# A gather-weighted adapter with residual and layer norm on one core: other shares of the b2 additions for three engines, and another order at the end

## The chip, the core and the metric

The kernel runs on one core of one Trainium2 chip. The core has five engines with a queue of instructions each: PE (TensorE, matmul), DVE (VectorE), ACT (ScalarE), GpSimd (POOL in the profile) and SP (SyncE, which here only issues transfers). They run side by side and wait for one another through semaphores. Sixteen DMA engines move data between device memory and the on-chip memory SBUF. Matmul results land in PSUM, a second on-chip memory of eight banks of 128 x 512 float32 values. The metric is the device time of one execution in microseconds. The kernel before takes 311.26 us (median of 3 runs, 311.04 to 311.28).

## What is computed

For each of 128 batches there is a block `x[b]` of 128 rows by 512 columns in float32, and a language number `v = itok[b]` from 0 to 8. Ten languages have their own weights.

```python
h       = relu(x[b] @ W1[v] + b1[v])             # 128 x 128
y       = x[b] + h @ W2[v] + b2[v]               # 128 x 512
mean    = mean of y over the 512 columns
var     = mean of (y - mean)^2 over the columns
out[b]  = x[b] + (y - mean) * rsqrt(var + 1e-5) * gamma[v] + beta[v]
```

All inputs and the output are float32.

## The kernel before

One batch fills the 128 partitions with its 128 rows. All weights stay in SBUF; at the start the rows of `beta`, `gamma` and `b2` are spread over all partitions by small matmuls (`spread`), so that `beta_b`, `gamma_b` and `b2_b` hold a 128 x 512 block for each language. Gamma is stored times -0.5, which the last step of the root below needs.

A batch passes through these steps, named by the functions of the code and the lines of the profile:

- `transpose_x` (L232, PE): four 128 x 128 transposes into the PSUM tile `pxT`; `copy_xT` (L236, ACT) brings it to SBUF.
- `stage_w1` (L223, ACT) copies the batch's W1 into the tile `w1s`; `down` (L255, PE) multiplies; `relu` (L263, ACT) makes `hT`.
- `up` (L272, PE) multiplies with W2 into the PSUM tile `py`, one of five buffers.
- `b2` is added in one of three ways. `add_b2` (L242, GpSimd) writes `r = x + b2` ahead of time, into a ring of four SBUF tiles. Or `vector_b2` (L282, DVE) adds it to `py` in PSUM. Or `up` puts a small matmul in front (L271, PE) that starts `py` with the b2 row. `b2_by_matmul(b)` and `b2_by_vector(b)` decide; what neither takes goes to GpSimd.
- `residual` (L289, DVE) adds `r` or `x` to `py`, with the row sums as a second result; `negative_means` (L303, DVE) turns the sums of two batches into means.
- `square` (L312, ACT) takes the sum of squared deviations, and `deviation` (L322, ACT) an approximate reciprocal root of it, for two batches at once. `rstd` (L326, L328, L331, DVE) refines that root by one Newton step in three small instructions.
- `scale` (L355, DVE): `py = (py - mean) * gamma`, and `finish` (L364, DVE): `o = py * rstd + o`, where `add_beta` (L249, GpSimd) has put `o = x + beta` before. Finishing a batch frees its `py` buffer for the batch five later.
- `store` (L368, SP) writes two batches.

The order is written out by hand: `keep` chains every instruction behind the one before it on its engine, so each engine runs exactly in program order. In the main loop, iteration `i` works on several batches at once: PE transposes batch `i`, runs `down` for `i - 1` and `up` for `i - 2`; DVE takes the residual of `b = i - 3`, finishes batch `b - 3` and scales batches of the pair before; GpSimd makes `r` for `b + 2` and `o` for `b`.

All roots lie in one PSUM tile, `small`: columns 0 and 1 are zeros, which `negative_means` adds as its second operand, and other columns take the roots of two pairs in turn and of the last four single batches. The framework tracks what waits for what by tiles.

The last batches go another way. `E` is 123; from batch 124 on `tail(b)` writes out the order by hand, with roots for single batches (`deviation_of`, L395 and L322; `rstd_of`, again L326, L328, L331). Batches 123 and 124, and the left half of 125, are finished by ACT and GpSimd together (`by_pool`: ACT at L409 computes `py * rstd`, with the mean's part from `shift`, L403, as bias where gamma is still to come; GpSimd multiplies by gamma at L411 and adds `o` at L413). The rest is finished by DVE (`finish_cols`, L420). All of GpSimd's remaining beta additions stand ahead of its first `by_pool` instruction in its queue. The last six batches are stored one by one (`store_last`, L416), in the order 122 to 127 on SP's queue.

Of the kernel before, what the change touches and what calls it, by code (L numbers as in the profile page):

```python
# [8 lines left out]
FP = mybir.dt.float32  # L9
# [3 lines left out]
ALU = mybir.AluOpType  # L13
# [3 lines left out]
P = 128  # L17
G = 4
EPS = 1e-5
# [6 lines left out]
def cond_resid_kernel(ctx: ExitStack, tc: tile.TileContext, x, itok, W1, b1, W2, b2, gamma, beta, out):  # L26
# [8 lines left out]
    nc = tc.nc  # L35
    B, S, H = x.shape
# [8 lines left out]
    def keep(ins):  # L45

        engine = ins.ins.engine
        if engine in last:
            tc.add_manual_dep(ins.ins, last[engine], behind, reason="kept order")
        last[engine] = ins.ins.name  # L50
        return ins
# [4 lines left out]
    op = ctx.enter_context(tc.tile_pool(name="op", bufs=5))  # L56
    tp = ctx.enter_context(tc.tile_pool(name="tp", bufs=2))
    wp = ctx.enter_context(tc.tile_pool(name="wp", bufs=5))
    st = ctx.enter_context(tc.tile_pool(name="st", bufs=6))
    p_x = ctx.enter_context(tc.tile_pool(name="p_x", bufs=1, space=PSUM))  # L60
    p_h = ctx.enter_context(tc.tile_pool(name="p_h", bufs=1, space=PSUM))
    p_s = ctx.enter_context(tc.tile_pool(name="p_s", bufs=1, space=PSUM))
# [3 lines left out]
    E = B - 5  # L66
# [6 lines left out]
    def xb(b):  # L73
        return xs[b // G][:, b % G, :]
# [57 lines left out]
    def lid(b, engine):  # L132
        g = b // G
        if (g, engine) not in lids:
            loads, vals = nc.values_load_multi_w_load_instructions(
                lang[0:1, g * G : (g + 1) * G],
                engines=[engine],
                min_val=0,
                max_val=L - 1,
                skip_runtime_bounds_check_because="clamped on the chip to 0..L-1 above",  # L140
            )
            for ins in loads:
                keep(ins)
            lids[g, engine] = vals
        return lids[g, engine][b % G]
# [65 lines left out]
    xT, hT, rs, os, ys, ssqs, nmeans, rstds = {}, {}, {}, {}, {}, {}, {}, {}  # L211
    phs, pxs, sums = {}, {}, {}

    def b2_by_matmul(b):
        return b < 4 or (b % 4 == 1 and not b2_by_vector(b) and b < E)

    def b2_by_vector(b):
        return b % 4 == 1 and (b % 8 == 5 if b < 24 else b % 32 != 1) and 8 <= b < B - 8

    def stage_w1(b):  # L220
        w1s[b] = wp.tile([P, KC, A], FP, tag="w1s", name=f"w1s_{b}")
# [53 lines left out]
    def col(tiles, b):  # L275

        return tiles[b // 2][:, b % 2 : b % 2 + 1]
# [6 lines left out]
    def residual(b):  # L284
        r = rs.pop(b) if b in rs else xb(b)
        if b % 2 == 0:
            sums[b // 2] = st.tile([P, 2], FP, tag="sum", name=f"sum_{b // 2}")
        keep(
            nc.vector.scalar_tensor_tensor(ys[b], ys[b], 1.0, r, ALU.mult, ALU.add, accum_out=col(sums, b))  # L289
        )  # L290


    small = {}

    def smalls(lo, n):
        if not small:
            small["t"] = p_s.tile([P, 64], FP, tag="s", name="small")
            keep(nc.vector.memset(small["t"][:, 0:2], 0.0))
        return small["t"][:, lo : lo + n]

    def negative_means(g):
        nmeans[g] = st.tile([P, 2], FP, tag="nmean", name=f"nmean_{g}")
        keep(nc.vector.scalar_tensor_tensor(nmeans[g], sums[g], -1.0 / H, smalls(0, 2), ALU.mult, ALU.add))  # L303

    def square(b):

# [10 lines left out]
    H3 = float(H) ** 3  # L317
# [3 lines left out]
    def root(ssq, t):  # L321
        keep(nc.scalar.activation(t, ssq, AF.Abs_reciprocal_sqrt, bias=eps, scale=1.0 / H3))  # L322

    def newton(n, ssq, t, u):
        if n == 1:
            keep(nc.vector.scalar_tensor_tensor(u, ssq, EPS * H3, t, ALU.add, ALU.mult))  # L326
        else:
            keep(nc.vector.scalar_tensor_tensor(u, u, 1.0 / H3, t, ALU.mult, ALU.mult))  # L328

    def newton_3(rstd, t, u):  # L330
        keep(nc.vector.scalar_tensor_tensor(rstd, u, -3.0, t, ALU.add, ALU.mult))  # L331

    parts_of = {}

    def of_pair(g):
        if g not in parts_of:
            parts_of[g] = smalls(8 + 8 * (g % 2), 2), st.tile([P, 2], FP, tag="part", name=f"part_{g}")
        return parts_of[g]

    def deviation(g):  # L340
# [2 lines left out]
    def rstd(g, n):  # L343
        t, u = of_pair(g)
        if n < 3:
            newton(n, ssqs[g], t, u)
        else:
            rstds[g] = st.tile([P, 2], FP, tag="rstd", name=f"rstd_{g}")
            newton_3(rstds[g], t, u)
            del ssqs[g], parts_of[g]  # L350

    def scale(b):
        v = lid(b, ET.DVE)
        keep(
            nc.vector.scalar_tensor_tensor(  # L355
                ys[b], ys[b], col(nmeans, b), gamma_b[:, bass.ds(v * H, H)], ALU.add, ALU.mult
            )
        )

    def finish(b):  # L360
        g, j = divmod(b, 2)
        o = os[g][:, j, :]
        keep(
            nc.vector.scalar_tensor_tensor(o, ys.pop(b), rstds[g][:, j : j + 1], o, ALU.mult, ALU.add)  # L364
        )

    def store(g):
        keep(nc.sync.dma_start(out=out[2 * g : 2 * g + 2].rearrange("b s h -> s b h"), in_=os.pop(g)))  # L368
        del rstds[g]
# [5 lines left out]

    shifts = {}

    def of_one(b):
        if -b not in parts_of:
            parts_of[-b] = smalls(32 + 8 * (b % 4), 1), st.tile([P, 1], FP, tag="part", name=f"part_of_{b}")  # L380
        return parts_of[-b]

    def rstd_of(b, n):

        t, u = of_one(b)
        if n < 3:
            newton(n, ssqs[b], t, u)
        else:
            rstds[b] = st.tile([P, 1], FP, tag="rstd", name=f"rstd_{b}")
            newton_3(rstds[b], t, u)  # L390

    def deviation_of(b):
        ssqs[b] = st.tile([P, 1], FP, tag="ssq", name=f"ssq_{b}")
        sq = tp.tile([P, H], FP, tag="sq", name=f"sq_{b}")
        keep(nc.scalar.activation(sq, ys[b], AF.Square, bias=col(sums, b), scale=-float(H), accum_out=ssqs[b]))  # L395
        root(ssqs[b], of_one(b)[0])

    def rstd_col(b):
        return rstds[b] if b > E else rstds[b // 2][:, b % 2 : b % 2 + 1]

    def shift(b):
        shifts[b] = st.tile([P, 1], FP, tag="shift", name=f"shift_{b}")
        keep(nc.vector.tensor_scalar(shifts[b], col(nmeans, b), rstd_col(b), None, ALU.mult))  # L403

    def by_pool(b, scaled, cols=slice(0, H)):

        n = rp.tile([P, H], FP, tag="r", name=f"n_{b}")[:, cols]
        bias = 0.0 if scaled else shifts[b]
        keep(nc.scalar.activation(n, ys[b][:, cols], AF.Identity, bias=bias, scale=rstd_col(b)))  # L409
        if not scaled:  # L410
            keep(nc.gpsimd.tensor_tensor(n, n, gamma_b[:, bass.ds(lid(b, ET.Pool) * H, H)], ALU.mult))  # L411
        o = os[b // 2][:, b % 2, cols]
        keep(nc.gpsimd.tensor_tensor(o, n, o, ALU.add))  # L413

    def store_last(b):
        nc.sync.dma_start(out=out[b], in_=os[b // 2][:, b % 2, :])  # L416

    def finish_cols(b, cols=slice(0, H)):
        o = os[b // 2][:, b % 2, cols]
        keep(nc.vector.scalar_tensor_tensor(o, ys[b][:, cols], rstd_col(b), o, ALU.mult, ALU.add))  # L420

    def tail(b):
        p = E // 2
        residual(b)
        if b == E + 1:
            rstd(p, 1)
            scale(E - 1)
            rstd(p, 2)
            finish(E - 2)
            store(p - 1)  # L430
            rstd(p, 3)
            deviation_of(b)
            shift(E)
            by_pool(E, False)
        elif b == E + 2:
            rstd_of(b - 1, 1)
            negative_means(b // 2)
            rstd_of(b - 1, 2)
            finish_cols(E - 1)
            store_last(E - 1)  # L440
            rstd_of(b - 1, 3)
            store_last(E)
            deviation_of(b)
        elif b == E + 3:
            left, right = slice(0, H // 2), slice(H // 2, H)
            shift(b - 2)
            by_pool(b - 2, False)
            residual(b + 1)
            store_last(b - 2)
            rstd_of(b - 1, 1)  # L450
            scale(b - 1)
            rstd_of(b - 1, 2)
            negative_means(b // 2)
            deviation_of(b)
            scale(b)
            rstd_of(b - 1, 3)
            deviation_of(b + 1)
            by_pool(b - 1, True, left)
            rstd_of(b, 1)
            scale(b + 1)  # L460
            rstd_of(b, 2)
            finish_cols(b - 1, right)
            store_last(b - 1)
            rstd_of(b, 3)
            rstd_of(b + 1, 1)
            finish_cols(b)
            store_last(b)
            rstd_of(b + 1, 2)
            rstd_of(b + 1, 3)
            finish_cols(b + 1)  # L470
            store_last(b + 1)
# [46 lines left out]
    for i in range(3, B + U):  # L518
        b = i - U - 1
# [25 lines left out]
        g, half = divmod(b, 2)  # L545
# [80 lines left out]
```

## Time and profile before

| | |
|---|---|
| median of 3 runs | 311.26 us |
| the profiled execution's own time | 311.25 us |
| its span in the profile | 309.4 us |
| PE busy | 298.0 us, 1845 instructions |
| DVE busy | 296.2 us, 827 |
| ACT busy | 280.1 us, 716 |
| GpSimd busy | 281.4 us, 235 |
| b2 by GpSimd (L242) | 94 batches, mean 1279 ns |
| b2 by DVE (L282) | 23 batches, mean 692 ns |
| b2 by PE (L271) | 11 batches, mean 380 ns |
| moved by the DMA engines | 77.58 MB, mean 251 GB/s |

Times in the profile are microseconds from the span's start. A line of the timeline has the start, the duration, the engine, the source line, the operation, what it writes and reads by the program's names, and in brackets how long the engine was idle before it and what ended that. Instructions of one engine can overlap a little: a duration runs to the last write, and the next instruction starts earlier, so the distance from start to start is what an instruction costs its engine. A line of the list of waits has the engine and line that waited, what it waited for, and then the sum in us, the number of times and the longest. PEld is PE's loading of weights, which overlaps the matmuls; POOL is GpSimd; SPq is SP's queue of transfers.

### The profile page before, as it was taken

The numbers are of one execution on the slowest core, as the hardware profiler recorded it, in microseconds if no ns is written. First come the engines' busy times: TensorE is split into PE (matmuls) and PEld (weight loads), VectorE is DVE, ScalarE is ACT, GpSimd is POOL, SyncE is SP. The second block draws the span as 40 slices with busy tenths as digits, with TensorE's granted clock in tenths as the row PEclk, the third lists the DMA queues.
The fourth block names the chain that finished last, engine by engine and source line by source line (L and its number), as shares of the span: only waits on it lengthen the run. The fifth ranks groups of instructions, "written<-read, shape, count | busy, mean of one in ns | idle before, by whom it ended". The sixth has DMA issues, their size and how long they took to land. (4 is left out here: it accounts for less than half of the span.)

```text
span 309.4 us, 6966 instructions
## 1 busy us (share of the span) xinstructions
PE 298.0 (96%) x1845; PEld 222.1 (72%) x1845; DVE 296.2 (96%) x827; ACT 280.1 (91%) x716; POOL 281.4 (91%) x235
## 2 busy tenths in 40 slices
PE   8999999999999999999999999999999999999970
PEld 3758778787777777777777777777777777777740
DVE  6787999999999999999999999999999999999994
ACT  3857999999999999999999999999999999999991
POOL 1349999999999999999999999999999999999893
PEclk9999999999999999999999999999999999999995
DMA  7999979986677766666876766677765766882244
GB/s 232 390 387 387 374 225 370 375 278 232 230 271 267 243 210 225 222 233 239 271 249 219 246 202 246 228 250 271 249 225 203 244 237 222 263 271 106 111 159 170
DMA packets 43481, 77.58 MB, mean 251 GB/s; under 512 B 1930, under 2 KB 7061, under 8 KB 43443
## 3 DMA queue, kind: packets, MB, share of 16 engines
q1 hardware_dynamic: 43382, 77.10, 71.9%
q8 instruction: 15, 0.25, 0.3%
q14 instruction: 24, 0.19, 0.2%
q10 hardware_dynamic: 60, 0.05, 0.1%
HBM read 43.58 MB, written 33.55 MB: 249 GB/s over the span
## 5 line engine op out<-in xcount | busy, mean ns | idle before, releaser
L249 POOL TENSOR_TENSOR o<-x,beta_b 128x512 f32<-128x512 f32 x128 | 162.2, 1279 | 9.4 <-DVE beta_b L209 9.4
L255 PE MATMUL ph<-xT,w1s 128*128 128x128 f32 x1024 | 135.4, 275 | 0.0
L242 POOL TENSOR_TENSOR r<-x,b_b 128x512 f32<-128x512 f32 x94 | 120.2, 1279 | 13.1 <-DVE b_b L209 6.2
L272 PE MATMUL py<-w,hT 128*128 x256 | 132.0, 598 | 0.0
L255 PEld LDWEIGHTS ph<-xT,w1s 128*128 128x128 f32 x1024 | 124.9, 192 | 1.0 <-ACT hT L263 0.5
L232 PEld LDWEIGHTS pxT<-ident,x 128*128 128x128 f32 x512 | 66.6, 152 | 65.3 <-issue 35.4
L355 DVE SCALAR_TENSOR_TENSOR py<-py,nmean,gamma_b 128x512 f32<-128x512 f32 x126 | 95.0, 754 | 0.1
L364 DVE SCALAR_TENSOR_TENSOR o<-py,rstd,o 128x512 f32<-128x512 f32 x122 | 91.0, 746 | 0.0
L312 ACT ACTIVATE sq<-py,sum 128x512 f32<-128x512 f32 x124 | 85.2, 687 | 6.1 <-DVE py L289 6.1
L232 PE MATMUL pxT<-ident,x 128*128 128x128 f32 x512 | 78.0, 275 | 0.0
L236 ACT COPY xT<-pxT 128x512 f32<-128x512 f32 x128 | 75.1, 587 | 1.2 <-PE pxT L232 1.2
L289 DVE SCALAR_TENSOR_TENSOR py<-py,r 128x512 f32<-128x512 f32 x94 | 65.1, 693 | 1.4 <-PE py L272 0.7
L223 ACT COPY w1s<-w 128x512 f32 x104 | 63.6, 612 | 0.1
L263 ACT ACTIVATE hT<-ph,b1T 128x128 f32<-128x128 f32 x128 | 47.4, 370 | 6.4 <-PE ph L255 4.3
L272 PEld LDWEIGHTS py<-w,hT 128*128 128x128 f32 x256 | 39.6, 191 | 2.8 <-issue 0.9
L312 ACT ACTIVATION_READ_ACCUMULATOR sq<-py,sum 128x1 f32 x124 | 25.6, 206 | 0.0
L289 DVE SCALAR_TENSOR_TENSOR py<-py,x 128x512 f32<-128x512 f32 x34 | 23.8, 699 | 1.4 <-issue 0.8
L322 ACT ACTIVATE small<-ssq,eps 128x2 f32<-128x2 f32 (+1 forms) x66 | 17.5, 265 | 2.3 <-DVE nmean L303 0.2
L282 DVE TENSOR_TENSOR py<-py,b_b 128x512 f32<-128x512 f32 x23 | 15.9, 692 | 0.0
L289 DVE DVE_READ_ACCUMULATOR py<-py,r 128x1 f32 x94 | 13.3, 142 | 0.0
L326 DVE SCALAR_TENSOR_TENSOR part<-ssq,small 128x2 f32<-128x2 f32 x62 | 9.4, 152 | 1.8 <-ACT small L322 1.8
L223 ACT COPY w1s<-w1e 128x512 f32 x16 | 9.8, 613 | 1.2 <-DMA w1e<-in_L_cond_W_dram 1.1
(54 smaller groups left out, 97.4 us busy)
## 6 DMA issues: line engine op xcount, KB each, us to landing
out_dram<-o SPq DMA_DIRECT2D x61, 512.0 KB, 3.3
x<-in_x_dram SPq DMA_DIRECT2D x29, 1024.0 KB, 6.3
x<-in_x_dram SPq DMA_DIRECT2D x6, 512.0 KB, 8.9
w1e<-in_L_cond_W_dram SPq DMA_DIRECT2D x2, 1280.0 KB, 11.6
w<-in_L_cond_W_dram SPq DMA_DIRECT2D x4, 640.0 KB, 7.5
w1s<-in_L_cond_W_dram SPq DMA_DIRECT2D x8, 256.0 KB, 8.4
w<-in_L_cond_W_dram SPq DMA_DIRECT2D x1, 1792.0 KB, 10.1
out_dram<-o SPq DMA_DIRECT2D x6, 256.0 KB, 2.0
```

Of the source, the lines that this page charges most:

```text
L223: keep(nc.scalar.copy(w1s[b].rearrange("p k a -> p (k a)"), src))
L232: keep(nc.tensor.transpose(pxs[b][:, k, :], cols, ident))
L236: keep(nc.scalar.copy(xT[b], pxs.pop(b)))
L242: keep(nc.gpsimd.tensor_tensor(rs[b], xb(b), b2_b[:, bass.ds(v * H, H)], ALU.add))
L249: keep(nc.gpsimd.tensor_tensor(os[g][:, j, :], xb(b), beta_b[:, bass.ds(v * H, H)], ALU.add))
L255: nc.tensor.matmul(phs[b], lhsT=w1s[b][:, k, :], rhs=xT[b][:, k, :], start=(k == 0), stop=(k == KC - 1))
L263: keep(nc.scalar.activation(hT[b], phs.pop(b), AF.Relu, bias=b1T[:, bass.ds(lid(b, ET.Activation), 1)]))
L272: keep(nc.tensor.matmul(ys[b], lhsT=hT[b], rhs=w2[:, bass.ds(v * H, H)], start=not m, stop=True))
L289: nc.vector.scalar_tensor_tensor(ys[b], ys[b], 1.0, r, ALU.mult, ALU.add, accum_out=col(sums, b))
L312: nc.scalar.activation(sq, ys[b], AF.Square, bias=col(sums, b), scale=-float(H), accum_out=col(ssqs, b))
L355: nc.vector.scalar_tensor_tensor(ys[b], ys[b], col(nmeans, b), gamma_b[:, bass.ds(v * H, H)], ALU.add, ALU.mult)
L364: nc.vector.scalar_tensor_tensor(o, ys.pop(b), rstds[g][:, j : j + 1], o, ALU.mult, ALU.add)
```

## The change

The change has four parts.

1. Who adds b2. Batches 49, 81 and 113 go from DVE to GpSimd, and batch 17 goes from PE's small matmul to GpSimd. Before: 94 batches by GpSimd, 23 by DVE, 11 by PE; after: 98, 20 and 10.
2. The tile `small` and its zeros are gone. `negative_means` bypasses its second operation, and its second operand, which has to be named, is now the first two columns of the pair's second `py`. The roots of a pair get a PSUM tile of their own, from one buffer.
3. The last four batches' roots lie in SBUF tiles of their own, and their Newton steps are instructions with one tensor input and the root as a per-partition scalar.
4. At the end (`b == E + 3`, with `b` = 126) the residual of 127 stands ahead of the shift of 124; ACT squares 126 before its pass of 124 in `by_pool`, and takes the root of 126 after it; the square of 127 and the first Newton step of 126 stand a little earlier in the text.

```diff
     def b2_by_matmul(b):
-        return b < 4 or (b % 4 == 1 and not b2_by_vector(b) and b < E)
+        return b < 4 or (b % 4 == 1 and not b2_by_vector(b) and b % 32 != 17 and b < E)

     def b2_by_vector(b):
-        return b % 4 == 1 and (b % 8 == 5 if b < 24 else b % 32 != 1) and 8 <= b < B - 8
+        return b % 4 == 1 and (b % 8 == 5 if b < 24 else b % 16 != 1) and 8 <= b < B - 8
...
-    small = {}
-    def smalls(lo, n):
-        if not small:
-            small["t"] = p_s.tile([P, 64], FP, tag="s", name="small")
-            keep(nc.vector.memset(small["t"][:, 0:2], 0.0))
-        return small["t"][:, lo : lo + n]
     def negative_means(g):
         nmeans[g] = st.tile([P, 2], FP, tag="nmean", name=f"nmean_{g}")
-        keep(nc.vector.scalar_tensor_tensor(nmeans[g], sums[g], -1.0 / H, smalls(0, 2), ALU.mult, ALU.add))
+        keep(
+            nc.vector.scalar_tensor_tensor(
+                nmeans[g], sums[g], -1.0 / H, ys[2 * g + 1][:, 0:2], ALU.mult, ALU.bypass
+            )
+        )
...
     def of_pair(g):
-            parts_of[g] = smalls(8 + 8 * (g % 2), 2), st.tile([P, 2], FP, tag="part", name=f"part_{g}")
+            parts_of[g] = p_s.tile([P, 2], FP, tag="s", name=f"root_{g}"), st.tile([P, 2], FP, tag="part", name=f"part_{g}")
...
     def rstd_of(b, n):
-        t, u = of_one(b)
-        if n < 3:
-            newton(n, ssqs[b], t, u)
-        else:
-            rstds[b] = st.tile([P, 1], FP, tag="rstd", name=f"rstd_{b}")
-            newton_3(rstds[b], t, u)
+        r = roots[b]
+        t = st.tile([P, 1], FP, tag="part", name=f"part_{n}_of_{b}")
+        a, add, factor = ((ssqs[b], EPS * H3, None), (rstds.get(b), None, 1.0 / H3), (rstds.get(b), -3.0, None))[n - 1]
+        op, value = (ALU.mult, factor) if add is None else (ALU.add, add)
+        keep(nc.vector.tensor_scalar(t, a, value, r, op, ALU.mult))
+        rstds[b] = t

-    def deviation_of(b):
+    def deviation_of(b, between=lambda: None):
...
-        root(ssqs[b], of_one(b)[0])
+        between()
+        roots[b] = st.tile([P, 1], FP, tag="root", name=f"root_of_{b}")
+        root(ssqs[b], roots[b])
...
         elif b == E + 3:
             left, right = slice(0, H // 2), slice(H // 2, H)
+            residual(b + 1)
             shift(b - 2)
-            by_pool(b - 2, False)
-            residual(b + 1)
+            deviation_of(b, lambda: by_pool(b - 2, False))
             store_last(b - 2)
             rstd_of(b - 1, 1)
             scale(b - 1)
             rstd_of(b - 1, 2)
             negative_means(b // 2)
-            deviation_of(b)
             scale(b)
+            deviation_of(b + 1)
             rstd_of(b - 1, 3)
-            deviation_of(b + 1)
+            rstd_of(b, 1)
             by_pool(b - 1, True, left)
-            rstd_of(b, 1)
             scale(b + 1)
             rstd_of(b, 2)
```

More of the change, by code (lines that the diff above doesn't have):

```diff
@@ L376, in cond_resid_kernel @@
     shifts = {}
[L378 to L381, printed above, removed]
+    roots = {}
     def rstd_of(b, n):
-        t, u = of_one(b)
-        if n < 3:
-            newton(n, ssqs[b], t, u)
-        else:
-            rstds[b] = st.tile([P, 1], FP, tag="rstd", name=f"rstd_{b}")
-            newton_3(rstds[b], t, u)
-    def deviation_of(b):
+        r = roots[b]
[5 more added lines that the diff above has]
+    def deviation_of(b, between=lambda: None):
         ssqs[b] = st.tile([P, 1], FP, tag="ssq", name=f"ssq_{b}")
```

## The prediction

> **What bounds the kernel now.** I read the page's first section, then stretches of the timeline of PE, DVE and GpSimd, then the waits, then the last 10 us of every engine and of the DMA engines.
>
> ```profile
> PE 298.0 (96%) x1845; PEld 222.1 (72%) x1845; DVE 296.2 (96%) x827; ACT 280.1 (91%) x716; POOL 281.4 (91%) x235
> ```
>
> No engine stands out by busy time, so the pace has to be read from start to start. PE in the middle of the run, one batch after another:
>
> ```profile
> 147.94 0.60 PE L232 MATMUL pxT<-ident,x 128*128 128x128 f32 x4
> 148.38 1.06 PE L255 MATMUL ph<-xT,w1s 128*128 128x128 f32 x8
> 149.34 1.12 PE L272 MATMUL py<-w,hT 128*128 x2
> 150.31 0.60 PE L232 MATMUL pxT<-ident,x 128*128 128x128 f32 x4
> ```
>
> From 150.31 the next transposes start at 152.50, 154.69 and 156.88: 2.19 us per batch, matmul behind matmul. The step shown is 2.37: `up` starts late. From the transposes of batch 24 (66.31) to those of 127 (294.58) are 228.27 us; 103 steps of 2.191 and four b2 matmuls of 0.22 make 226.55. So PE waited 1.72 us, mostly in ten steps of about 0.17. The late `up(b)` starts 0.05 us after `finish(b-5)` ends on DVE, whose PSUM buffer it takes: DVE holds PE up there. Why, DVE shows:
>
> ```profile
> 154.75 0.75 DVE L364 SCALAR_TENSOR_TENSOR o<-py,rstd,o 128x512 f32<-128x512 f32 x1
> 155.41 0.69 DVE L282 TENSOR_TENSOR py<-py,b_b 128x512 f32<-128x512 f32 x1
> 156.01 0.15 DVE L331 SCALAR_TENSOR_TENSOR rstd<-part,small 128x2 f32<-128x2 f32 x1
> ```
>
> Residuals 58 and 62 start at 149.21 and 158.14: four batches, one with b2 on DVE, take 8.93, against PE's 4 x 2.191 = 8.76. Each such group puts DVE 0.17 further behind. A group without that add is 0.66 shorter (residual to residual 2.80 with it, 2.14 without): 8.27. DVE catches up there; otherwise PE waits from the fourth group on (51, 55, 59, 63; 83 to 95; 115, 119).
>
> GpSimd goes at 1.233 us from start to start (busy 1.279, overlapping), and waits only for its `r` buffers:
>
> ```profile
> POOL r L242 <- DVE part L326: 5.8, 20, 0.8
> ...
> DVE part_of L326 <- ACT small L322: 0.5, 1, 0.5
> ```
>
> Each wait ends 0.83 after the start of the residual that read the buffer four `r` tiles earlier. GpSimd is 8 to 9 us ahead of the residuals. The end:
>
> ```profile
> 291.40 1.27 POOL L242 TENSOR_TENSOR r<-x,b_b 128x512 f32<-128x512 f32 x1 [0.81 <-DVE part L326]
> ...
> 295.10 3.74 POOL L249 TENSOR_TENSOR o<-x,beta_b 128x512 f32<-128x512 f32 x3
> 298.78 1.28 POOL L411 TENSOR_TENSOR n<-n,gamma_b 128x512 f32<-128x512 f32 x1
> 300.14 1.27 POOL L413 TENSOR_TENSOR o<-n,o 128x512 f32<-128x512 f32 x1
> 301.36 1.27 POOL L411 TENSOR_TENSOR n<-n,gamma_b 128x512 f32<-128x512 f32 x1
> 302.71 1.94 POOL L413 TENSOR_TENSOR o<-n,o 128x512 f32<-128x512 f32 x2
> ```
>
> After its last wait (291.40) GpSimd has no gap to its end at 304.65. Its results are stores 123, 124 and half of 125. SP issues the last four stores at 304.00, 304.68, 305.10 and 306.10, and then:
>
> ```profile
> 304.85:307.70 2.85, 0.00 (x0) 0.00 (x0) 1.07 (x4) 0.00 (x0) 0.00 (x0) 0.50 0.95 364
> 307.70:309.40 1.70, 0.00 (x0) 0.00 (x0) 0.00 (x0) 0.00 (x0) 0.00 (x0) 0.50 0.00 0
> ```
>
> The second last column is the DMA share: 1 MB goes out in 2.85 us at 95%. So the chain of waits, which ends in DVE's finish(127) (to 306.07, store at 306.10), hides a second chain just as long: GpSimd, store 124, four full stores in a row.
>
> **b2 of 17, 49, 81 and 113 goes to GpSimd.** For DVE three adds go (49, 81, 113): 3 x 0.66 = 2.0 us. For PE the b2 matmul of 17 goes: 0.22. Over 32 batches DVE now needs 6 x 8.93 + 2 x 8.27 = 70.12, PE 32 x 2.191 + 0.22 = 70.33. After each third DVE-add group comes one without, and after three groups `up` still has 0.15 before it would wait (batch 79 in the trace). So PE's waits go: 1.72 + 0.22 = 1.94 us at PE's last matmul, and DVE, which at 123 to 127 follows PE by its least distance (0.70), comes 1.94 earlier into the end. ACT has 0.2 to 0.3 us of idle time per pair and follows.
>
> For GpSimd it is 4 x 1.233 = 4.93 us more. It waited 7.22 between `r_10` (32.64, set by a load) and its last beta add `o_127` (297.56): (297.56 - 32.64) - 209 x 1.233. Four more steps need four more gaps, and these lie elsewhere now. `r_50` cannot start before residual(46) + 0.83: (122.39 - 0.22) + 0.83 = 123.00. 57 steps later comes `r_82`, at 193.28 by its own pace, 193.35 by its buffer (residual 78 at 193.42, 0.90 earlier); 57 steps on `r_114`, at 263.63 and 263.68 (residual 110 at 264.44, 1.59 earlier). From there 27 steps without a wait: `o_127` at 263.68 + 33.29 = 296.97, only 0.59 earlier than before. The residuals never wait for it: its lead of 8 us shrinks by 2.8 at most (`r_50`: 2.55 later than before, its residual 0.22 earlier). But at the end, where PE and DVE come 1.94 earlier, GpSimd comes 0.59 earlier.
>
> **The means' second operand.** Same instruction, same 128x2, again one SBUF and one PSUM operand; no row has a bypassed operand. From below: it can't go under 0.06 from start to start, which it has. From above: the pointer operand of L355 makes 0.06 of difference to L289. I take zero, the row itself. The memset (0.06 at 22.12) lies before the `w1e` load that releases ACT at 31.26: nothing. ACT's root no longer waits for the means (0.2 once), and a single PSUM tile for all roots adds no wait: the square before each root already waits for a residual that DVE runs after the last reader.
>
> **Newton steps by scalar, roots in SBUF.** Twelve steps of L326, L328, L331 (0.15 each, 0.06 to 0.07 to the next start) become a tensor_scalar with a pointer. The nearest row is the shift:
>
> ```profile
> 299.50 0.21 DVE L403 TENSOR_SCALAR shift<-nmean,rstd 128x1 f32<-128x1 f32 x1
> ```
>
> 0.21, and 0.12 to the next start (297.12 to 297.25): 0.06 more each, 0.7 in all as the upper bound; zero is the lower one. Three hide in the gap before residual(127), which waits for PE (299.75). The others put DVE back by about 0.4. Against this, 0.45 goes: with all roots in one tile `part_of(126)` waited for the root of 127, and with tiles of its own it doesn't. Sum for finish(127): -0.05. The shift row lies inside a GpSimd instruction (298.78 to 300.06) and neither is longer than its like. The Trainium skill (SBUF — State Buffer, Who interferes with whom) speaks against such steps: a tensor_scalar with all operands in SBUF can take the port pair shared with GpSimd, and the second to come is blocked for the other's whole length. By that rule each of the nine late steps could stand up to 1.27 us, some 5 us in all if half of that is met; by the shift row it is nothing, and I go by the row.
>
> **Ends reordered.** residual(127) moves ahead of shift(124), and ACT squares 126 before `n` of 124. So `n` of 124 comes 0.87 later against PE, ready at 301.45 - 1.94 = 299.5. GpSimd reaches it at 301.36 - 0.59 = 300.77: hidden by 1.2 us of GpSimd's own queue. DVE ends at 306.07 - 1.94 - 0.05 = 304.1.
>
> **The sum.** GpSimd's end moves by 0.59. Store 124: 304.00 to 303.41; 125 (its half by GpSimd) 304.09; SP's pitch of 0.42 makes 126 at 304.5 and 127 at 305.0, before their turn. The four stores' data run from 304.26 for about 2.8 us to 307.1, where 307.70 was before: 0.6 us. That is what is left of 1.94. The profiled execution took 311.25 (span 309.4), the median is 311.26: 311.25 - 0.6 = 310.6.
>
> **Rivals.** (1) The whole gain of PE and DVE arrives, or most: 309.3 to 309.9. It needs a GpSimd that is quicker than its 1.233, or stores that overlap better than 95%. All 213 steps speak against it. (2) Slower: the bypassed form costs DVE more. Sixteen means per 32 batches against a margin of 70.33 - 70.12 = 0.21: from 0.013 us each DVE sets the pace again. At 0.06, the price of L355's pointer, DVE's 32 batches take 71.1, PE's waits return (71.0 now), only the 0.22 stays; then `r_114` starts at 264.44 - 0.22 + 0.83 = 265.05, `o_127` at 298.34, 0.78 later than before, and the stores behind it: 312.0. Nothing is gained below 0.033. No row shows such a price. (3) GpSimd's queue eats the rest: the Newton steps or a late load cost it 0.3 to 0.6 more, and the time stays at 310.9 to 311.4.
>
> **Numbers.** Forecast (310.3 to 310.95) 0.66; rival 1 0.12; rival 2 0.12, of which 0.04 under 0.2%; rival 3 0.10, of which 0.08 within. 0.2% (0.62 us, about what a measurement of this kernel can tell from no change) lies nearly on the forecast: just over half of it, 0.36, counts as faster. Faster 0.48, same 0.42, slower 0.10. Leaving out rival 1 below 310.0 and the dear end of rival 2: 310.0 to 311.5.
>
> **What would show it.** Right: ten of PE's long steps gone and its last matmul near 297.7; GpSimd's waits for `r` nearly gone after 130 us; its beta adds end near 298.2 and its end near 304.1; DVE ends near 304.1, some 0.9 before the last store is issued; the stores' DMA stretch ends near 307.1; the new steps at 0.21. Wrong: means over 0.165, PE still waiting, a GpSimd or DVE instruction of the end stretched by the other, or gaps in GpSimd's last 30 us.

## The result, and the profile after

The changed kernel takes 314.29 us (median of 4 runs, 314.27 to 314.49); the kernel before, on the same chip, 311.17 (4 runs, 311.04 to 311.28). The ratio is 1.0102, 95% interval 1.0084 to 1.0119: 3.1 us slower. The forecast was 310.6, range 310.0 to 311.5. The profiled execution took 314.27 us, with a span of 312.5.

The first section of the page after, to be held against the line shown of before:

```profile
PE 299.9 (96%) x1844; PEld 219.6 (70%) x1844; DVE 297.7 (95%) x823; ACT 278.4 (89%) x716; POOL 285.5 (91%) x239
```

It shows the shares moved as planned: GpSimd has four instructions more and 4.1 us more to do. It does not show where 3.1 us went. The list of waits does; its columns are engine and line that waited, what for, the sum in us, how often, the longest:

```profile
PEld pxT L232 <- ACT xT L236: 42.2, 100, 0.9
PEld pxT L232 <- issue: 26.7, 107, 0.3
ACT sq L308 <- DVE nmean L296: 10.2, 20, 0.5
...
POOL r L242 <- DVE part L322: 5.2, 4, 1.6
```

The lines of before that they stand against:

```profile
PEld pxT L232 <- issue: 35.4, 135, 0.3
PEld pxT L232 <- ACT xT L236: 28.5, 91, 0.9
...
ACT sq L312 <- DVE py L289: 6.1, 15, 2.0
POOL r L242 <- DVE part L326: 5.8, 20, 0.8
```

The third line of after is new. ACT's square waits for DVE's means, 20 times, 0.51 us each; before there was no such line. (The square waited then for the residual alone.) And the 20 are the batches whose b2 DVE still adds, one for one. The first line is what came of it: the weight loads of PE's transposes wait 42.2 us in all for `copy_xT`, against 28.5 before; with the waits named "issue" it is 68.9 against 63.9.

One such place in the timeline of DVE after, at batch 61 (start, duration, engine, line):

```profile
156.22 0.69 DVE L282 TENSOR_TENSOR py<-py,b_b 128x512 f32<-128x512 f32 x1
...
156.94 0.70 DVE L289 SCALAR_TENSOR_TENSOR py<-py,x 128x512 f32<-128x512 f32 x1
...
157.56 0.75 DVE L351 SCALAR_TENSOR_TENSOR py<-py,nmean,gamma_b 128x512 f32<-128x512 f32 x1
158.22 0.15 DVE L296 SCALAR_TENSOR_TENSOR nmean<-sum,py 128x2 f32<-128x2 f32 x1
```

and of ACT in the same two microseconds:

```profile
157.52 0.37 ACT L263 ACTIVATE hT<-ph,b1T 128x128 f32<-128x128 f32 x1
158.40 0.69 ACT L308 ACTIVATE sq<-py,sum 128x512 f32<-128x512 f32 x1 [0.51 <-DVE nmean L296]
...
159.93 0.57 ACT L236 COPY xT<-pxT 128x512 f32<-128x512 f32 x1
```

The same batch before (DVE, DVE, ACT):

```profile
156.14 0.70 DVE L289 SCALAR_TENSOR_TENSOR py<-py,x 128x512 f32<-128x512 f32 x1
...
157.42 0.15 DVE L303 SCALAR_TENSOR_TENSOR nmean<-sum,small 128x2 f32<-128x2 f32 x1
```

```profile
156.93 0.69 ACT L312 ACTIVATE sq<-py,sum 128x512 f32<-128x512 f32 x1 [0.34 <-DVE py L289]
```

After, the residual starts at 156.94 and its row sums are there by about 157.7. Before, the same square started 0.79 after its residual (156.14 to 156.93) and 0.49 ahead of the means. Here it starts 1.46 after it: first DVE does a `scale` of another pair (0.66 to the next start) and then the means, and only then the square may go. ACT is free from 157.89 on (157.52 and 0.37), 0.33 before the means start at 158.22: it waits for a read that has not begun, so what holds it is an order between the two instructions, not a clash of two reads that run at once. In the text of the program the order is residual, `scale`, means, `finish`, square. Behind the square ACT reads out its sum, takes the root, does `stage_w1` and then `copy_xT` at 159.93, which frees the one PSUM buffer that PE's next transposes write. PE after, the transposes alone:

```profile
158.18 0.60 PE L232 MATMUL pxT<-ident,x 128*128 128x128 f32 x4
...
160.55 0.65 PE L232 MATMUL pxT<-ident,x 128*128 128x128 f32 x4
...
162.80 0.60 PE L232 MATMUL pxT<-ident,x 128*128 128x128 f32 x4
```

The transposes at 160.55 start 0.62 after `copy_xT` did. The steps are 2.37 and 2.25 where 2.19 is PE's own: 0.24 lost for each batch whose b2 DVE adds. Of the 20, 19 lie between the transposes of batch 24 (66.21) and of 127 (297.23): 19 x 0.24 = 4.6. Counted from the ends it is the same: 231.02 less 103 x 2.191 and four b2 matmuls of 0.22 (33, 65, 97 and 121, as before) leaves 4.5 us of waiting, where 1.72 was before and none was forecast.

GpSimd hangs on the residuals through its ring, so it is late too:

```profile
267.47 1.28 POOL L242 TENSOR_TENSOR r<-x,b_b 128x512 f32<-128x512 f32 x1 [1.39 <-DVE part L322]
...
298.30 3.73 POOL L249 TENSOR_TENSOR o<-x,beta_b 128x512 f32<-128x512 f32 x3
...
305.90 1.94 POOL L408 TENSOR_TENSOR o<-n,o 128x512 f32<-128x512 f32 x2
```

`r_114`, forecast at 263.68, starts at 267.47, 3.8 later. From there 27 steps of 1.233 give 300.76 for `o_127`, the last of the three in the second line; it started at 300.77. So GpSimd ends 3.8 later than forecast (307.84 against 304.06), and that is what the time shows: 3.7 over the forecast. PE, whose last matmul ends at 302.30 where 297.7 was forecast, is 4.6 late. Store 124 is issued at 307.19 (304.00 before), and the last stretch of stores, in the table of windows (the second last column is the DMA share), ends 3.2 us later than before:

```profile
308.00:310.90 2.90, 0.00 (x0) 0.00 (x0) 0.66 (x1) 0.00 (x0) 0.00 (x0) 0.50 0.96 362
```

### The profile page after: what moved, and what is told of

Same layout as the page of the kernel before. It is cut to its first block, busy times and chain, and to the rows that moved or that the text cites. A ratio compares the mean times of both kernels' runs of the same rounds, so it can differ in the third digit from the quotient of the medians.

```text
span 312.5 us, 6895 instructions
## 1 busy us (share of the span) xinstructions
PE 299.9 (96%) x1844; PEld 219.6 (70%) x1844; DVE 297.7 (95%) x823; ACT 278.4 (89%) x716; POOL 285.5 (91%) x239
## 5 line engine op out<-in xcount | busy, mean ns | idle before, releaser
L242 POOL TENSOR_TENSOR r<-x,b_b 128x512 f32<-128x512 f32 x98 | 126.1, 1286 | 12.2 <-DVE b_b L209 6.3
L232 PEld LDWEIGHTS pxT<-ident,x 128*128 128x128 f32 x512 | 65.1, 152 | 71.2 <-ACT xT L236 42.2
L232 PE MATMUL pxT<-ident,x 128*128 128x128 f32 x512 | 79.1, 277 | 0.3
L289 DVE SCALAR_TENSOR_TENSOR py<-py,r 128x512 f32<-128x512 f32 x98 | 67.8, 692 | 2.8 <-PE py L272 0.7
L289 DVE SCALAR_TENSOR_TENSOR py<-py,x 128x512 f32<-128x512 f32 x30 | 21.0, 699 | 1.6 <-issue 0.9
L318 ACT ACTIVATE root<-ssq,eps 128x2 f32<-128x2 f32 x62 | 16.5, 265 | 2.1
L282 DVE TENSOR_TENSOR py<-py,b_b 128x512 f32<-128x512 f32 x20 | 13.8, 691 | 0.0
L322 DVE SCALAR_TENSOR_TENSOR part<-ssq,root 128x2 f32<-128x2 f32 x62 | 9.5, 153 | 1.7 <-ACT root L318 1.7
```

Source lines behind the costliest of these rows:

```text
L232: keep(nc.tensor.transpose(pxs[b][:, k, :], cols, ident))
L242: keep(nc.gpsimd.tensor_tensor(rs[b], xb(b), b2_b[:, bass.ds(v * H, H)], ALU.add))
```

## The experiments

The new operand makes DVE's means a reader of `py` of the pair's odd batch, in PSUM, and ACT's square reads the same `py` later in the program. The theory (A in the expectations): the later of the two readers, on another engine, waits for the earlier. Rivals: the means themselves became dearer; the shares or the end cost the time; the square waits because both instructions read the sums; the wait comes from where the instructions stand on their engines and not from their order in the text. Each ratio is to the kernel before, run on the same chip.

**1. The even batch's `py` as operand.** Its square stands ahead of the means in the program anyway.

```diff
-                nmeans[g], sums[g], -1.0 / H, ys[2 * g + 1][:, 0:2], ALU.mult, ALU.bypass
+                nmeans[g], sums[g], -1.0 / H, ys[2 * g][:, 0:2], ALU.mult, ALU.bypass
```

> The changed kernel with one index changed: the means' second operand is the first two columns of the pair's even py instead of its odd one. Theory A (two readers of one py buffer on different engines wait for one another, so the odd batch's square waits for the means): the square of the even batch is long over when the means run, so ACT's 10.2 us of waits on the means go, PE's steps of 2.36 and 2.25 go back to 2.19, and the time is what the prediction gave without that wait, 310.4 to 310.9. Rival B (the four batches more on GpSimd hold the run up): 314 as after. Rival C (the reordered end costs it): 314 as after. Rival D (the bypassed form itself is dearer): 314 as after.

310.79 us (11 runs), ratio 0.9989 (0.9980 to 0.9998). One index gives back 3.5 us. The square's wait for the means is gone from the list of waits, and PE's weight loads wait less for `copy_xT` than before the change (28.5):

```profile
PEld pxT L232 <- ACT xT L236: 22.3, 77, 1.0
```

The instruction is the same form on the same kind of operand (150 ns against 149), so its own price was not it. Means and square still both read the sums, so that was not it either.

**2. The means alone, on the kernel before.**

```diff
-        keep(nc.vector.scalar_tensor_tensor(nmeans[g], sums[g], -1.0 / H, smalls(0, 2), ALU.mult, ALU.add))
+        keep(nc.vector.scalar_tensor_tensor(nmeans[g], sums[g], -1.0 / H, ys[2 * g + 1][:, 0:2], ALU.mult, ALU.bypass))
```

> The kernel before with nothing changed but the means' second operand (odd py, bypassed); shares of b2, roots and end as before. Theory A: the odd square waits for the means in every pair, some 0.5 us where the batch has its b2 from DVE; groups with such a batch take PE 8.99 as after instead of 8.93, the group with a b2 matmul 8.98: 71.9 per 32 batches against 71.0, so about 3 us more, 313.8 to 314.8. Rival B and C: 311.2, no change. Rival D: 313 to 315, but with means instructions longer than 0.165 us.

314.92 us (4 runs), ratio 1.0116 (1.0100 to 1.0131), at the upper edge of what was expected.

```profile
ACT sq L312 <- DVE nmean L303: 11.9, 23, 0.6
...
POOL r L242 <- DVE part L326: 9.1, 23, 1.3
```

With the old shares DVE adds b2 for 23 batches, and there are 23 waits, at just these batches. The means took 150 ns each (151 before): the instruction is no dearer.

**3. The shares alone, on the kernel before** (the two lines of `b2_by_matmul` and `b2_by_vector`).

> The kernel before with nothing changed but the shares of b2 (17, 49, 81, 113 to GpSimd). Theory A and the prediction's sum: PE's waits for py buffers go, PE ends near 297.7, but GpSimd's last beta add starts only 0.6 us earlier (296.97) and the last four stores follow it: 310.5 to 310.9. If GpSimd's queue did not matter: 309.3. Rival B: 313 to 315. Rivals C and D: 310.5 to 310.9 as A.

310.54 us (11 runs), ratio 0.9980 (0.9971 to 0.9989). The end of GpSimd in its timeline:

```profile
294.35 3.75 POOL L249 TENSOR_TENSOR o<-x,beta_b 128x512 f32<-128x512 f32 x3
...
301.98 1.95 POOL L413 TENSOR_TENSOR o<-n,o 128x512 f32<-128x512 f32 x2
```

**4. The end alone, on the kernel before** (roots in SBUF, Newton steps by scalar, the new order).

> The kernel before with nothing changed but the last four batches (roots in SBUF tiles, Newton steps by per-partition scalar, the new order of the end); the means and the pairs' roots as before. Theory A: DVE's last instruction ends 0.05 earlier and GpSimd gets its tile of batch 124 about 0.15 later than it could take it, so 311.1 to 311.5. Rival C: 313 to 314.5. Rivals B and D: 311.2.

311.23 us (11 runs), ratio 1.0000 (0.9991 to 1.0009): nothing.

The parts add up: 0.9980 x 1.0116 x 1.0000 = 1.0096, inside the interval of the whole change. One part was not run alone: the pairs' roots in PSUM tiles of their own.

**5. Both readers in the other order.** In the changed kernel the odd batch's square is written right behind its residual, ahead of the means in the text. Each engine's own order stays as it was.

```diff
                 residual(b)
+                square(b)
...
-            square(b)
+            if half == 0:
+                square(b)
```

> The changed kernel (odd py as second operand) with the call of the odd batch's square written ahead of the means; the order on each engine is the same, only which of the two readers stands first in the program differs. Theory A (of two readers of one py buffer on different engines the later written waits for the earlier): the square's waits on the means go, and DVE's means wait for ACT's square instead, 0.25 to 0.4 us in each of some 60 pairs, on an engine that has 0.2 us to spare per 32 batches: 322 to 330. Rival E (the square waits for the means because both read the sums, or because the hardware holds two readers of a bank apart): no wait of the means, 310.5 to 311 or 314 as after.

332.31 us (4 runs), ratio 1.0671 (1.0652 to 1.0689), a little above the range expected.

```profile
DVE nmean L296 <- ACT sq L308: 17.7, 62, 2.1
PEld py L272 <- DVE o L360: 17.4, 25, 0.8
```

The wait has turned round: now DVE's means wait for ACT's square, 62 times. What decides is which reader comes first in the text; that two engines' queues are unchanged does not help. It is far dearer this way, since behind the means on DVE stands `finish`, which frees a `py` buffer, and PE's `up` waits for that (second line). The rival by the engines' own order falls.

**6. An operand in SBUF.** The means take `sums[g]` twice, so no second reader of `py` exists.

```diff
-                nmeans[g], sums[g], -1.0 / H, ys[2 * g + 1][:, 0:2], ALU.mult, ALU.bypass
+                nmeans[g], sums[g], -1.0 / H, sums[g], ALU.mult, ALU.bypass
```

> The changed kernel with the sums themselves, in SBUF, as the means' bypassed second operand. Theory A: the square has no reader of py in front of it, so the square's waits go, as in e1. Whether it then is as fast as e1 depends on the Trainium skill's rule (SBUF - State Buffer, Who interferes with whom), by which an instruction of DVE with two SBUF inputs and one of GpSimd that reads SBUF block one another: by the rule 64 means next to a GpSimd that is busy 97% of the time, up to 1.28 us each, so 320 or more; without it 310.4 to 310.9.

347.26 us (4 runs), ratio 1.1167 (1.1123 to 1.1210). The means' own line (after the count: shortest, median and longest in ns):

```profile
L296 DVE SCALAR_TENSOR_TENSOR nmean<-sum x64: 145/1050/1485, 22.4 to 337.5; 128x2 f32<-128x2 f32 x64
```

Two values per partition take up to 1.49 us, and DVE is busy 41.3 us longer with them (50.9 against 9.6 with the even `py`). A GpSimd instruction took 1.28 us in the same run, as ever. In the trace, 57 of the 64 start while a GpSimd instruction runs, and each of these ends 0.02 to 0.04 us after the end of one; the other seven take 0.15 to 0.16 us. So the means wait for GpSimd's instruction to end. It is what the Trainium skill (SBUF — State Buffer, Who interferes with whom) says of a DVE instruction with two inputs from SBUF beside a GpSimd instruction that reads SBUF; the run agrees, down to two elements. The operand may be ignored by the arithmetic, but its place is not ignored.

**7. Batch 113 back to PE's matmul.** With the wait gone, the sum of the prediction says that GpSimd's queue sets the end. So one batch is taken from GpSimd: first on the kernel with the even operand, then on the shares alone.

```diff
-        return b < 4 or (b % 4 == 1 and not b2_by_vector(b) and b % 32 != 17 and b < E)
+        return b < 4 or (b % 4 == 1 and not b2_by_vector(b) and (b % 32 != 17 or b == 113) and b < E)
```

> The kernel with the even operand (e1_even_operand), and batch 113's b2 by PE's small matmul instead of by GpSimd. Theory A with the prediction's second half (GpSimd's queue and the last four stores set the end): GpSimd has 1.233 us less, PE 0.22 more; PE's last matmul comes 0.22 later than in e1, o_127 about 1.2 earlier, the last four stores go out about 1.0 earlier: 309.5 to 310.0 where e1 took 310.79. Rival (the end is set by PE and DVE, GpSimd's queue is covered): 0.2 later than e1, 311.0.

310.23 us (6 runs), ratio 0.9966 (0.9954 to 0.9978): better, but by less than expected. `o_127` starts 0.89 earlier than in experiment 1 (296.55 against 297.44), and GpSimd then waits 0.21 for ACT's `n` of 124, so its end comes 0.6 earlier.

> The kernel before with the new shares of b2, except that batch 113 has its b2 by PE's small matmul; means, roots and end as before. By the same sum as for e5: GpSimd's end comes 1.83 earlier than before the change, PE's 1.72, the last stores with them: 309.4 to 309.8, below e3_shares_only (310.54). If GpSimd's queue is not what sets the end of e3: 310.7.

309.42 us (5 runs), ratio 0.9945 (0.9931 to 0.9958). It beats both kernels, by 1.8 us and 4.9 us. `o_127` starts at 295.48 instead of 296.82 in experiment 3, which is one step of 1.233 and 0.10, and the time falls by 1.12.

**8. What separates the last two?** The first has, beside the shares, the even operand, the pairs' roots in tiles of their own and the new end. The operand and the end were put alone on the best version.

> The shares with batch 113 by PE's matmul (309.42 us), and in addition only the means' second operand changed: bypassed, the first two columns of the pair's even py. Roots, Newton steps and the end's order as before the change. If the even operand by itself costs the 0.8 us by which the kernel with the even operand, the new roots and the new end (310.23) stands behind (the means now wait for ACT's square of the even batch, or a long PE step near batch 65 comes with it): 310.0 to 310.4, and PE's transposes of 127 near 293.6. If that operand is harmless, and the new end is what costs: 309.2 to 309.7, transposes of 127 near 292.6.

310.41 us (7 runs), ratio 0.9977 (0.9965 to 0.9988). It costs about what the first case gave, but not where: there is no long step near batch 65, and PE's transposes of 127 stand 0.4 later against its first ones (0.24 of it before batch 24). The rest is at the very end. DVE, and ACT beside it:

```profile
299.64 0.15 DVE L303 SCALAR_TENSOR_TENSOR nmean<-sum,py 128x2 f32<-128x2 f32 x1
300.64 0.76 DVE L355 SCALAR_TENSOR_TENSOR py<-py,nmean,gamma_b 128x512 f32<-128x512 f32 x1 [0.84 <-ACT sq L395]
```

```profile
299.83 0.69 ACT L395 ACTIVATE sq<-py,sum 128x512 f32<-128x512 f32 x1 [0.78 <-DVE nmean L303]
```

In the old end, `deviation_of(126)` is written behind the last pair's means. So here the even `py` falls into the same trap, once: the square waits 0.78 for the means, and the `scale` that overwrites `py` waits 0.84 for the square. DVE's last `finish` starts at 304.54, where it was 303.33. In the new end that square is written ahead of the means.

> The shares with batch 113 by PE's matmul (309.42 us), and in addition only the end: SBUF roots of the last four batches, their Newton steps by scalar, the new order. The means as before the change. If the new end costs nothing here, as it did alone (311.23 beside 311.23): 309.2 to 309.7. If it costs because GpSimd now waits for ACT's later n of 124 (with 113 off GpSimd its queue no longer hides the 0.87 us by which n of 124 moved back): 310.0 to 310.4, store 124 issued near 303.0 in place of 301.9, and a wait of GpSimd for n in its last 6 us.

309.69 us (4 runs), ratio 0.9949 (0.9932 to 0.9967), not to be told from 309.42. GpSimd waits once for ACT's later `n` of 124, 0.22 us. The difference of 0.27 is no larger than PE's lateness in this profile (transposes of 127 at 292.86 against 292.59, 0.24 of it before batch 24), so no price of the end reordered can be read from it.

So neither part explains by itself why the first kernel of experiment 7 stays 0.8 behind the second. In its profile PE is 1.02 late at the transposes of 127, counted from its first ones: 0.56 of that before batch 24, while the first loads arrive, 0.30 at batch 65, and 0.15 at 113. The profile puts the step at 65 down to the residual of 60, which waits 0.21 for GpSimd's `r` (the kernel of experiment 1 has the same step); but `r_60` had ended some 6 us before (146.82 against 153.07). What ends just before that residual, at 152.91, is a load of language numbers on DVE's queue. These loads, in the first kernel and in the second (count, then shortest, median and longest in ns):

```profile
L135 DVEq TENSOR_LOAD <-lang x32: 351/882/1702, 20.4 to 292.7; - x32
L135 DVEq TENSOR_LOAD <-lang x32: 346/594/1622, 20.4 to 291.5; - x32
```

They take 0.88 to 0.89 us in the median after batch 24 in the three kernels with the even operand, and 0.59 to 0.63 in all the others; why, the runs do not show. The pairs' roots in tiles of their own, the third difference, were not run alone. Whether the 0.56 belongs to that kernel or to that one execution stays open: the kernel of experiment 1 is 0.42 late there too, but all of it by batch 10, where this one is 0.16 late, and the kernels with the old means and roots differ by 0.3 there among themselves.

## Why the prediction was wrong

**The step that failed is "The means' second operand".** It asked what the instruction costs ("Same instruction, same 128x2, again one SBUF and one PSUM operand") and answered zero. As far as it went, that was right: 149 ns against 151. What it left out is that an operand is also an access, with an order to the other accesses of the same PSUM tile. The old operand, columns of `small`, was shared with nothing but the roots; the new one is a buffer that ACT's square reads next. The same step noticed that "ACT's root no longer waits for the means (0.2 once)", which was a wait of a like kind between the same two engines (ACT's write of a root behind DVE's read of the same tile), and did not look for the one that took its place. What the runs showed in place of the zero: 20 waits of the square, 0.51 us each, which are worth 3.5 us in the changed kernel (experiment 1) and, with 23 of them, 3.7 us by themselves (experiment 2; 3.6 by the ratio). That is the error of the forecast, 314.29 less 310.6, to within what these runs tell apart.

It could have been seen. The trace of before gives the slack: the square starts 0.79 after an odd residual behind a DVE add, ACT being idle for 0.34 before it; the means end about 1.4 after that residual. From those two rows it can be worked out that a square which waits for the means starts some 0.65 later in each of 20 batches, once one asks who else touches `py`; it came to 0.67 (1.46 less 0.79).

**"ACT has 0.2 to 0.3 us of idle time per pair and follows"** failed with it: 0.67 later is more than that idle time, so ACT became late and with it `copy_xT`, then PE.

**Rival 2** had the sign and the place (the means) but not the mechanism: a dearer instruction, which experiments 1 and 2 rule out. Its 312.0 was too low by 2.3 since it only put PE back to its old 1.72 us of waiting; what came is 4.5. Rivals 1 and 3 did not show: without the wait the time is within the forecast's 310.3 to 310.95 (310.79 in experiment 1, 310.54 in experiment 3).

**The shares: right, in each number of the sum, once the means are left alone** (experiment 3): last matmul 297.7 and 297.58; `r_50` 123.00 and 122.84; `o_127` 296.97 and 296.82; GpSimd's end 304.06 and 303.93; DVE's end 304.1 and 304.02; store 124 issued 303.41 and 303.27; the stores' data until 307.1 and 307.0; the time 310.6 and 310.54. All come 0.1 to 0.2 early, and that is luck: in that execution PE reached the transposes of batch 10 at 34.60, before at 34.75, ahead of the first batch (17) that the shares touch. GpSimd's lead over the residual of 50 shrank by 3.4, not by 2.8 at most (9.59 to 6.16): the residual came 1.05 earlier, not 0.22, and that cost nothing. The picture of two chains of the same length, of which the change shortens one by 1.94 and the other by 0.59, held. Experiment 7 confirms it from the other side: one GpSimd step less, 1.1 us less (0.6 on the kernel with the even operand).

**Newton steps by scalar: right.** Eight of the twelve new steps in the table of groups (207 is the mean in ns):

```profile
L382 DVE TENSOR_SCALAR part_of<-part_of,root_of 128x1 f32<-128x1 f32 x8 | 1.7, 207 | 0.0
```

The shift row had 210. None of the twelve was stretched (204 to 214 ns). The Trainium skill (SBUF — State Buffer, Who interferes with whom), which the prediction set against them, says that a `tensor_scalar` can contend with GpSimd when its operands meet the conditions of a two-port mode; the prediction left that condition out. The runs show only that steps on one value were not blocked. In experiment 4 DVE ends 0.23 earlier (305.84 against 306.07) behind a PE that ends 0.17 earlier (299.47 against 299.64): -0.06, where -0.05 was forecast, and nothing on the total.

**Ends reordered: right in effect** (experiment 4), with a limit that the prediction gave (1.2 us of GpSimd's queue) and that experiment 8 reached: with one step less GpSimd came 1.3 us earlier than in experiment 3, met the later `n`, and waited 0.22.

## What to carry to other kernels

When an operand is replaced by something that "does not matter", price three things: the instruction, the memory that the operand lies in, and every other access of that tile, above all on other engines and further down in the text. A dummy operand should be a tile that nobody else is waiting to use. The hand-tuned order here left a few tenths of a microsecond of slack at the hand-over (0.34 ahead of the square shown); a new wait of 0.5 us in 20 of 128 batches cost more here than the instruction could, and an average of busy time does not show it: the list of waits does, in one line.

## What the runs showed that was not expected

- Two reads of one PSUM buffer by DVE and ACT do not run side by side here: the later in the text waits for the earlier (20 waits of 0.51 us after; 62 the other way round in experiment 5), and it waits even while the earlier has not begun. In SBUF this did not show: means and square both read the sums in every kernel, and where `py` is not shared no such wait is listed. Which part of the system asks for the order, the runs do not show.
- A DVE instruction on 128 x 2 values with both inputs in SBUF took 1.05 us in the median beside GpSimd's tensor additions, against 0.15 with one of them in PSUM: it ended when GpSimd's instruction did. GpSimd's own (1.28 us) were not longer for it.
- A `tensor_scalar` on one value per partition with all operands in SBUF took 0.21 us beside the same GpSimd work, with nothing added.
